# A two-layer graph attention kernel: VectorE's order beside the products of W1 is dealt anew, two weight sums trade places, a third of each W2 block is loaded earlier, and the last logit rows go into four column groups

## The chip, the core and the metric

The kernel runs on one core of a Trainium2 chip. Its metric is the time of one execution in device microseconds (us). Before the change it is 633.82 us, the median of three runs (633.66 to 633.97). The profile shown here is that of one further execution. Engines are named as in the profile: PE is TensorE (PEld its weight loads), DVE is VectorE, ACT is ScalarE, POOL is GpSimd, SP is SyncE.

## What is computed

The reference is a graph attention network of two layers over 512 nodes and 8704 edges, with a residual and a layer norm. Cut to what matters:

```python
def gat_layer(x, W, a_s, a_d, b, edge_index, concat):
    h = (x @ W).reshape(n, H, C)
    alpha_s = einsum('nhc,hc->nh', h, a_s)
    alpha_d = einsum('nhc,hc->nh', h, a_d)
    e = leaky_relu(alpha_s[src] + alpha_d[dst], 0.2)
    e = exp(e - segment_max(e, dst)[dst])
    alpha = e / (segment_sum(e, dst)[dst] + 1e-16)
    return segment_sum(h[src] * alpha[:, :, None], dst) + b
h = elu(gat_layer(x, W1, a_src1, a_dst1, b1, edges, concat=True))   # 8 heads of 768
out = gat_layer(h, W2, a_src2, a_dst2, b2, edges, concat=True)      # 1 head of 768
y = layernorm(x + out)
```

x is 512x768, W1 768x6144 (8 heads of 768 columns) and W2 6144x768 (8 blocks of 768 rows), all in float32. The numbers of edges between each pair of nodes are counted into a dense 512x512 matrix first; after that the attention is dense.

## The kernel before, in words

**Stages.** The whole kernel is one function, `gat_pass`, and the order of its instructions is written by hand: each engine runs its own list in the order in which the lines are emitted, and waits on semaphores where it needs another engine. After the counting and the first projections (up to about 92 us of the trace) a loop `for h in range(H - 1)` goes over the heads 0 to 6. For each head it emits three stages, and PE runs them one behind the other:

1. `mixed(h, ...)` (matmuls on L966): the attention matrix times head h's features, by a seven-product scheme (P1 to P7) in three columns `c`; the result goes through `elu` into gT.
2. The second product: gT times the block of W2 of head h, added into h2. For h = 0 it is `by_halves` (seven products P1 to P7 in two parts, matmuls on L409, emptied on L445 to L451); from h = 1 it is `second_by_thirds`, 15 products of 8 recorded matmuls each (matmuls on L480, emptied on L486, L491 and L493).
3. The product of x and the block of W1 of head h + 2: `by_halves` for h = 0, `project_by_thirds` for h = 1 to 5, again 15 products on L480. I call this the **third stage**. There is none for h = 6.

The last head, 7, has its own `last_mixed` (L1008), then `second` (L409), then the attention of the second layer (L1384 to L1451), and the last loop (L1472) that forms the output rows and normalises them.

**Products that share a bank.** The two 15-product schemes keep five PSUM banks, one for each chain a, x, b, y, z (`STEPS`, L455 to L458). A product adds to what stands in its chain's bank, so it may start only when the step before it on that chain has been read out (`empty`, ACT on L486 or DVE on L493). In the third stage, counted from n = 0, the order is P8 P13 P9 P2 P4 P12 P6 P0 P1 P10 P5 P14 P11 P7 P3; P14 (n = 11) and P7 (n = 13) lie on chain x, P11 (n = 12) and P3 (n = 14) on chain y. In the second product the order is P13 P2 P8 P4 P12 P9 P6 P0 P1 P14 P10 P5 P11 P7 P3, with P10 (n = 10) and P11 (n = 12) on chain y.

**What DVE does beside the products.** In the loop of the third stage (L1308 to L1327) DVE gets, between `multiply` and `empty` of product n: the sums of W1 (`sums[p]`, L170), the left and right sums of the next attention product (`sums3`, L928 to L931 and L939 to L942), two pairs of logits (`logits`, a pair of 768-wide multiply-and-accumulate instructions on L424, at n = 11 and n = 13), and the sums P2 (n = 12) and P6 (n = 14) of the next W2 block (`sums2`, L170). The sum P4 of that block was done in the third column of the next head's `mixed` (`amid`, L1241). For h = 1 alone there are also sums of x: P13 and P9 (L1076, L1073) go beside products 8 and 10 of the second product (`in_second`, L1276), P12 and P5 beside products 2 and 7 of the third stage.

**Loads of W2.** `load_second` (L197 to L210) brings a block of W2: SP loads the rows by chunks (`load_rows(k)`, six DMAs of 384 KB), and POOL issues DMAs that add (`add_up`, L133). POOL issues in order, and each waits until what it adds to has landed. The order was: rows 1, P1 added to, rows 2, P14 added to, P0, P11, P10; the last, P10, adds P1 on top and so waits for P1. P6 is P14 - P4 and P1 is P6 + P1, so DVE's P1 waits for P10 to have read its old value.

**The last logit rows.** h2's logits for the second layer come in two parts: V times gT (`add_rows` on L1384, K = 128, 2 output columns of weights, 512 moving columns, six of them over chunks c) and the logits of h2 itself, turned by a product with the identity (four of 128 columns). `rows[32 * j:32 * j + 2]` with `tile_position=(0, 32 * j)` puts such a product in the column group j of the PE array; a product with `picks` (L1416, L1418) later sums all four groups. Before, the six went to groups 0 to 2 and the four all to group 2; the bank is cleared by a memset (L1394) that `last_mixed` emits in its column c = 1.

Of the kernel before, what the change touches and what calls it, by code (L numbers as in the profile page):

```python
# [37 lines left out]
def gat_pass(  # L38
# [16 lines left out]
    nc = tc.nc  # L55
    P = 128
# [3 lines left out]
    NT = N // P  # L60
    DC = D // P
# [70 lines left out]
    def add_up(o, i):  # L132
        nc.gpsimd.dma_start(o, i, accum_op=ALU.add)  # L133
# [63 lines left out]
    def load_second(h):  # L197

        B_, part, load_rows, load_pairs, load_four, ops = thirds_of(w2[h * D:(h + 1) * D, :], "w1", w1_sums.get, w1_rows)

        def load_rest():
            load_rows(1)
            add_up(B_["P1"], part(1, 2))
            load_rows(2)
            add_up(B_["P14"], part(0, 1))
            add_up(B_["P0"], B_["P12"])
            load_four("P11", "P10")
            add_up(B_["P10"], B_["P1"])
        ops["P7"] = lambda: add_up(B_["P7"], B_["P6"])
        return B_, ops, load_pairs, lambda: load_rows(0), load_rest  # L210
# [71 lines left out]
    ident = const.tile([P, P], F32, name="ident")  # L282
# [90 lines left out]
    V = keep.tile([P, DC, 2], F32, name="V")  # L373
# [48 lines left out]
    def logits(h, feats, t):  # L422
        for al, a, sign in zip(AL[h], A[h], (1.0, -1.0)):
            nc.vector.scalar_tensor_tensor(scr, feats[:, t, :], sign, a, op0=ALU.mult,  # L424
                                           op1=ALU.mult, accum_out=al[:, t:t + 1])
# [745 lines left out]
    for h in range(H - 1):  # L1171
# [14 lines left out]
        if h == 0:  # L1186
# [25 lines left out]
            for n in range(2, 7):  # L1212
                (m0, e0), (m1, e1) = pairs[2 * n:2 * n + 2]
                m0()
                m1()
                if n < 6:
                    scored(n - 2)
                if n < 5:
                    score(n - 1)
                if n == 6:  # L1220
                    turn_in(0)
                    out_by_dma(2)
                e0()
                if 3 < n < 6:
                    out_by_dma(n - 4)
                if n == 6:
                    out_by_dma(3)
                    B2, sums2, load_pairs, load_first, load_rest = load_second(1)
                    load_pairs()
                    load_first()  # L1230
                    load_rest()
                e1()
                if n < 5:
                    fold_count(n - 1)
        else:
            G, gsums = g_thirds(h)

            def of_b(*names):
                return [sums2.pop(p) for p in names if p in sums2]

            amid = [[], of_b("P6", "P2"), behind] if h == 1 else [of_b("P1"), [], of_b("P4")]  # L1241
            finish = mixed(h, AA, BB, [[[sources[0]], [sources[1]] + amid[0]], [row, [targets[0]] + amid[1]], [amid[2], [targets[1]]]],
                           [gsums[p] for p in ("P13", "P8")])
            behind = []
# [28 lines left out]
            def also(n, *what):  # L1273
                plan[n] = plan.get(n, []) + list(what)

            for n, f in zip((8, 10), in_second):  # L1276
                also(n, f)
            if not last:
                for f in attend:
# [25 lines left out]
        if 0 < h and not last:  # L1305
            pairs = project_by_thirds(h + 2, XB, B3)
            AA, sums3 = left_sums(h + 1)
            for n in range(15):  # L1308
                pairs[n][0]()
                for p in {0: ("P6", "P2"), 1: ("P4",), 4: ("P10",), 5: ("P0",), 6: ("P1",), 9: ("P7",),  # L1310
                          12: ("P3",)}.get(n, ()):
                    sums[p]()
                if n == 5:
                    BB, rsums_ = right_sums()
                    sums3 += rsums_
                if n in (2, 3, 5, 6, 8, 9, 10):
                    for _ in range(2 if n == 8 else 1):
                        sums3.pop(0)()
                if n in (11, 13):
                    logits(h + 2, HS[h + 2], 2 + (n - 11) // 2)  # L1320
                if n in in_third:
                    in_third.pop(n)()
                if n in (12, 14):
                    sums2.pop("P2" if n == 12 else "P6")()
                pairs[n][1]()
                if n in (1, 2, 4):
                    turn_in((n + 2) // 2)  # L1327
            assert not sums3
        elif not last:
            B_, sums = right(W1[h + 2], "w2")  # L1330
            pairs = projection(h + 2, XA, B_)
            for n in range(14):
                pairs[n][0]()
                if n == 0:
                    for f in attend:
                        f()
                if n in (1, 3):
                    sums[n // 2]()
                if n == 1:
                    AA, sums3 = left_sums(h + 1)  # L1340
                pairs[n][1]()
                if n in (1, 2, 4):
                    turn_in((n + 2) // 2)
                if n == 5:
                    BB, sums3 = right_sums()
                if 1 <= n < 9:
                    sums3.pop(0)()
                if n == 0:
                    XB, early, store, late_ = x_thirds()
                if n in (2, 3, 5, 6, 7, 8, 9):  # L1350
                    early.pop(0)()
                if n == 9:
                    store()
                if n in (10, 12):
                    logits(h + 2, HS[h + 2], 2 + (n - 10) // 2)
                if n == 13:
                    late_["P10"]()
                    behind = [late_["P8"]]
                    in_second, in_third = [late_["P13"], late_["P9"]], {2: late_["P12"], 7: late_["P5"]}
        else:  # L1360
            B2, additions = sums_by_dma(W2[H - 1], w2[(H - 1) * D:, :], "w1")
            additions[0]()
            last_sum()
            additions[1]()
# [18 lines left out]
    def add_rows(lhsT, rhs, j, cols, start, stop):  # L1383
        nc.tensor.matmul(rows[32 * j:32 * j + 2, cols], lhsT, rhs, start=start, stop=stop,  # L1384
                         tile_position=(0, 32 * j), skip_group_check=True)
# [5 lines left out]

    first, second_, third_, fourth = (given(t) for t in range(NT))
    BB, rsums = right_sums()
    finish = last_mixed(AA, BB, [*rsums, lsums[3]], {(1, 0): [lambda: nc.vector.memset(rows, 0.0)], (2, 0): second_[:1], (2, 1): first})  # L1394
    every = slice(0, N)
    pairs = second(GA, B2)

# [2 lines left out]
            f()  # L1400

    run(pairs[0][0], pairs[0][1], pairs[1][0], pairs[1][1], *finish, gsums[0], gsums[1], pairs[2][0], pairs[2][1])
    for c in range(DC):
        add_rows(V[:, c, :], gT[:, c, :], c % 3, every, c < 3, c > 2 and c % 3 != 2)
    run(second_[1], pairs[3][0], gsums[2], pairs[3][1], *third_, pairs[4][0], *fourth, pairs[5][0], pairs[4][1], pairs[5][1], gsums[3],
        pairs[6][0])
    for t in range(NT):
        add_rows(al2[:, :, t], ident, 2, slice(t * P, (t + 1) * P), False, t == NT - 1)
    row2 = work.tile([P, N], F32, name="nr")
    nc.scalar.copy(row2, rows[:, :N])  # L1410
    fold(parts[:2])
# [114 lines left out]
```

## Time and profile before

| | |
|---|---|
| time, median of three runs | 633.82 us |
| time of the profiled execution | 633.37 us |
| its span, first to last instruction | 631.6 us |
| mean granted clock of TensorE | 0.996 |
| stage `mixed` of a head (h = 2 to 6) | 18.13 us |
| second product and third stage of a head (h = 2 to 5) | 52.29 us to 52.30 us together |
| second product of the last layer (`second`, from L409) to the end | 571.6 to 631.6 us |

The page of the profile gives each engine's busy time, then its share in 40 slices of the span, then the chain of work that ended last and the costliest groups. A row of the timeline has the start (us from the span's start), the time until the last of its instructions ends, the engine, the line, the operation, what it writes and reads, the shape, how many instructions it merges (xN), and in brackets the idle time of the engine before it and who ended it. Each float32 product on PE is recorded as two matmuls. PE's ends are modelled and overlap the next start, so a wait of PE is read from the starts of two rows better than from idle time.

### The profile page before, as it was taken

The page shows a single profiled execution, that of the slowest core. Times are in us where ns is not written, and L with a number is a line of the kernel's source. Part 1 is how long each engine was busy: PE and PEld are TensorE (multiplying, and loading weights), DVE is VectorE, ACT ScalarE, POOL GpSimd, SP SyncE. Part 2 cuts the span into 40 slices and gives each one's busy share as a digit, 9 for nine tenths or more (in the row PEclk, how much of TensorE's full clock was granted, in tenths as well). Part 3 has the DMA queues.
Part 4 walks back from the last instruction along what each step waited for, and adds up shares of the span by engine and source line. Part 5 has one row for each costly group of instructions (what it writes and reads, how often), then busy time and mean ns, then how long its engine had stood idle before and what let it go on. Part 6 is the DMA issues. An engine that isn't in the chain of part 4 may idle for free.

```text
span 631.6 us, 8545 instructions
## 1 busy us (share of the span) xinstructions
PE 620.3 (98%) x2761; PEld 483.1 (76%) x2761; DVE 529.3 (84%) x1129; ACT 336.7 (53%) x598; POOL 149.2 (24%) x177
## 2 busy tenths in 40 slices
PE   8999999999999999999999999999999999999995
PEld 5555576556888888888888888888888888885553
DVE  8979989888898889968898778968897878968685
ACT  5875776650658236651658146751758146754361
POOL 1300011023333224323342422323342413010000
PEclk9999999999999999999999999999999999999998
DMA  8994397789999998999999998999999994590042
GB/s 292 329 245 96 70 259 249 173 244 258 246 205 152 320 253 186 181 271 222 254 214 179 310 251 182 187 290 224 226 213 202 304 279 88 124 249 2 17 76 78
DMA packets 109568, 129.45 MB, mean 205 GB/s; under 512 B 41622, under 2 KB 90446, under 8 KB 108750
## 3 DMA queue, kind: packets, MB, share of 16 engines
q1 hardware_dynamic: 75518, 91.35, 47.2%
q0 software_dynamic: 33568, 36.90, 37.7%
q10 hardware_dynamic: 432, 0.59, 0.3%
q8 instruction: 24, 0.39, 0.3%
q14 instruction: 26, 0.21, 0.1%
HBM read 99.84 MB, written 2.90 MB: 163 GB/s over the span
## 4 chain that ended last, share of the span: by engine, by line
PE 88%; DVE 5%; DMA 4%; ACT 1%; issue 1%; SPq 1%; DVEq 0%; POOLq 0%; ACTq 0%
PE mm L480 42%; PE mm L966 17%; PE mm L409 17%; PE mm L1472 3%; DMA w2r<-in_L_gnn_W_dram 3%; PE mm L1008 3%; PE held L409 2%; PE tr L742 1%; DMA w2t<-in_L_gnn_a_dst_dram 1%; PE bc L276 1%; PE held L608 1%; PE bc L742 1%; DVE h L493 0%; PE tr L1384 0%; DVE q L645 0%
## 5 line engine op out<-in xcount | busy, mean ns | idle before, releaser
L486 ACT ACTIVATE hs<-mm 128x512 f32<-128x512 f32 x30 | 17.9, 596 | 89.3 <-PE mm L480 71.2
L966 PE MATMUL mm<-PT,hs 128*128 128x256 f32 x252 | 61.3, 379 | 0.0
L493 DVE TENSOR_TENSOR hs<-hs,mm 128x512 f32<-128x512 f32 x45 | 30.8, 685 | 27.6 <-PE mm L480 27.6
L966 PEld LDWEIGHTS mm<-PT,hs 128*128 128x128 f32 x252 | 47.8, 190 | 7.2 <-ACT u L970 0.3
L649 ACT ACTIVATE q<-q,nmax 128x512 f32<-128x512 f32 x32 | 23.1, 721 | 52.9 <-DVE nmax L645 52.8
L491 POOL DMA_DIRECT2D h<-pass x22 | 26.5, 1319 | 84.4 <-ACT pass L490 75.5
L493 DVE TENSOR_TENSOR h<-h,mm 128x512 f32<-128x512 f32 x56 | 38.3, 684 | 6.2 <-PE mm L480 5.7
L966 PE MATMUL mm<-pS,gS 128*128 128x256 f32 x168 | 43.1, 379 | 0.0
L903 ACT COPY PT<-zr 128x1024 uint16<-128x1024 uint16 x34 | 39.2, 1155 | 1.5 <-DMA zr<-pS 0.9
L480 PE MATMUL mm<-w2r,gT 128*128 128x256 f32 x160 | 37.9, 385 | 0.0
L480 PE MATMUL mm<-w2r,xT 128*128 128x256 f32 x160 | 37.8, 379 | 0.0
L133 POOL DMA_DIRECT2D w1t<-in_L_gnn_W_dram x18 | 29.4, 1658 | 29.5 <-DMA w1t<-in_L_gnn_W_dram 28.7
L966 PEld LDWEIGHTS mm<-pS,gS 128*128 128x128 f32 x168 | 31.9, 190 | 4.3
L480 PE MATMUL mm<-w1t,hs 128*128 128x256 f32 x144 | 34.2, 380 | 0.5 <-DVE h L493 0.5
L480 PEld LDWEIGHTS mm<-w2r,gT 128*128 128x128 f32 x160 | 29.6, 190 | 6.6 <-DVE hs L493 3.0
L480 PE MATMUL mm<-w1r,gS 128*128 128x256 f32 x144 | 34.0, 379 | 0.0
L480 PE MATMUL mm<-w1r,hs 128*128 128x256 f32 x144 | 34.0, 379 | 0.0
L480 PEld LDWEIGHTS mm<-w2r,xT 128*128 128x128 f32 x160 | 30.4, 190 | 4.1
L970 ACT COPY u<-mm 128x256 f32<-128x256 f32 x21 | 7.8, 371 | 45.7 <-PE mm L966 45.7
L480 PEld LDWEIGHTS mm<-w1t,hs 128*128 128x128 f32 x144 | 27.2, 190 | 4.7 <-DVE h L493 0.9
L716 DVE TENSOR_SCALAR os<-nodes,idx 128x512 bf16<-128x512 f16 x104 | 29.2, 355 | 1.4 <-PE tr L742 1.4
L480 PEld LDWEIGHTS mm<-w1r,gS 128*128 128x128 f32 x144 | 27.3, 190 | 3.7
(295 smaller groups left out, 1566.6 us busy)
## 6 DMA issues: line engine op xcount, KB each, us to landing
w2r<-in_L_gnn_W_dram SPq DMA_DIRECT2D x48, 384.0 KB
w1r<-in_L_gnn_W_dram SPq DMA_DIRECT2D x43, 384.0 KB
gT<-xd SPq DMA_DIRECT2D x5, 1280.0 KB
w1t<-in_L_gnn_W_dram SPq DMA_DIRECT2D x24, 256.0 KB
h<-pass POOLq DMA_DIRECT2D x22, 256.0 KB, 4.3
w1t<-in_L_gnn_W_dram POOLq DMA_DIRECT2D x18, 256.0 KB, 6.0
w2t<-in_L_gnn_W_dram SPq DMA_DIRECT2D x15, 256.0 KB
w2t<-in_L_gnn_W_dram POOLq DMA_DIRECT2D x15, 256.0 KB, 8.9
```

Of the source, the lines that this page charges most:

```text
L133: nc.gpsimd.dma_start(o, i, accum_op=ALU.add)
L409: nc.tensor.matmul(ps[:, :HALF], A_[p][:, k, i * P:(i + 1) * P], B_[p][:, k, :], start=start and k == 0, stop=k == HK - 1, skip_group_chec ...
L480: nc.tensor.matmul(bank[chain][:, i * TH:(i + 1) * TH], A_[p][:, k, i * P:(i + 1) * P], B_[p][:, k, :], start=first and i == k == 0, stop= ...
L486: nc.scalar.activation(out(o), ps, AF.Copy, scale=sign)
L491: nc.gpsimd.dma_start(out(o), part, accum_op=ALU.add)
L493: nc.vector.tensor_tensor(out(o), out(o), ps, op=ALU.add if sign > 0 else ALU.subtract)
L649: nc.scalar.activation(q, q, AF.Exp, bias=nmax, scale=-1.0, accum_out=dens[t])
L716: nc.vector.tensor_scalar(o, nodes, idx[:, c:c + 1], None, op0=ALU.is_equal)
L903: nc.scalar.copy(PT.rearrange("p s n -> p (s n)").bitcast(U16).rearrange("p (s n h) -> p s n h", s=NT, h=2)[:, :, t * P:(t + 1) * P, :], p ...
L966: nc.tensor.matmul(bank[p][:, :HN], A_[p][:, k, c * P:(c + 1) * P], B_[p][:, k, :], start=over is None and k == 0, stop=k == 1, skip_group ...
L1008: nc.tensor.matmul(banks[c, p][:, :HN], A_[p][:, k, c * P:(c + 1) * P], B_[p][:, k, :], start=over is None and k == 0, stop=k == 1, skip_g ...
L1472: nc.tensor.matmul(ps[:, :cols.stop - cols.start], PT[:, s, t * P:(t + 1) * P], h2[:, s, cols], start=(s == 2), stop=(s == 1))
```

## The change

No product, no transfer and no vector operation is added or taken away, except that two of the six rows of V are cut in halves; the rest is order and place.

- **Loads of W2** (`load_second`): rows 2 and the addition to P14 come ahead of rows 1 and the addition to P1.
- **h = 0, second product**: at n = 3 the first half's `empty` (L448) is emitted ahead of the ranking of the attention rows (`scored(1)`) instead of behind it.
- **P4 of the next W2 block** is no longer in `mixed`'s third column; it is the last thing of the third stage, behind P6.
- **h = 1**: the two sums of x beside the second product go from products 8 and 10 to 12 and 14.
- **Third stage**: the two left sums go to n = 1 and the others to n = 2, 6, 7, 8, 9 (before: 2, 3, 5, 6, 8, 8, 9, 10); the sums P7 and P3 of W1 go from n = 9 and 12 to 8 and 10; P2 of the next W2 block goes from n = 12 to 3, and P6 stays at 14; the four logit instructions go one each to n = 11, 12, 13, 14 (before: two at 11, two at 13).
- **Last layer**: the memset of the rows moves from `last_mixed`'s column 1 ahead of its columns, behind the sums; one logit instruction of h2's rows 128 to 255 moves from column 2 to the end of column 1; the rows of V go four whole ones to groups 0 to 3 and the two others as four halves of 256 columns to groups 0 to 3; the four turned logits go one to each group.

```diff
         def load_rest():
+            load_rows(2)
+            add_up(B_["P14"], part(0, 1))
             load_rows(1)
             add_up(B_["P1"], part(1, 2))
-            load_rows(2)
-            add_up(B_["P14"], part(0, 1))
             add_up(B_["P0"], B_["P12"])
...
                 m0()
                 m1()
+                if n == 3:
+                    e0()
                 if n < 6:
                     scored(n - 2)
...
-                e0()
+                if n != 3:
+                    e0()
...
-            amid = [[], of_b("P6", "P2"), behind] if h == 1 else [of_b("P1"), [], of_b("P4")]
+            amid = [[], of_b("P6", "P2"), behind] if h == 1 else [of_b("P1"), [], []]
...
-            for n, f in zip((8, 10), in_second):
+            for n, f in zip((12, 14), in_second):
...
+            some = [f for t in (2, 3) for f in half_logits(h + 2, t)]
             for n in range(15):
                 pairs[n][0]()
-                for p in {0: ("P6", "P2"), 1: ("P4",), 4: ("P10",), 5: ("P0",), 6: ("P1",), 9: ("P7",),
-                          12: ("P3",)}.get(n, ()):
+                for p in {0: ("P6", "P2"), 1: ("P4",), 4: ("P10",), 5: ("P0",), 6: ("P1",), 8: ("P7",),
+                          10: ("P3",)}.get(n, ()):
                     sums[p]()
...
-                if n in (2, 3, 5, 6, 8, 9, 10):
-                    for _ in range(2 if n == 8 else 1):
-                        sums3.pop(0)()
-                if n in (11, 13):
-                    logits(h + 2, HS[h + 2], 2 + (n - 11) // 2)
+                for _ in range({1: 2, 2: 1, 6: 1, 7: 2, 8: 1, 9: 1}.get(n, 0)):
+                    sums3.pop(0)()
+                for f in {11: some[:1], 12: some[1:2], 13: some[2:3], 14: some[3:]}.get(n, ()):
+                    f()
                 if n in in_third:
                     in_third.pop(n)()
-                if n in (12, 14):
-                    sums2.pop("P2" if n == 12 else "P6")()
+                for p in {3: ("P2",), 14: ("P6", "P4")}.get(n, ()):
+                    sums2.pop(p)()
                 pairs[n][1]()
...
-    finish = last_mixed(AA, BB, [*rsums, lsums[3]], {(1, 0): [lambda: nc.vector.memset(rows, 0.0)], (2, 0): second_[:1], (2, 1): first})
+    finish = last_mixed(AA, BB, [*rsums, lsums[3], lambda: nc.vector.memset(rows, 0.0)], {(1, 1): second_[:1], (2, 1): first})
...
-    for c in range(DC):
-        add_rows(V[:, c, :], gT[:, c, :], c % 3, every, c < 3, c > 2 and c % 3 != 2)
+    for c in range(4):
+        add_rows(V[:, c, :], gT[:, c, :], c, every, True, False)
+    for j in range(4):
+        c, cols = 4 + j // 2, (near, far_)[j % 2]
+        add_rows(V[:, c, :], gT[:, c, cols], j, cols, False, False)
...
     for t in range(NT):
-        add_rows(al2[:, :, t], ident, 2, slice(t * P, (t + 1) * P), False, t == NT - 1)
+        add_rows(al2[:, :, t], ident, t, slice(t * P, (t + 1) * P), False, True)
```

## The prediction

> **What bounds the kernel now.** I read the page first, then the chain of work that ended last, then the timelines of PE and DVE around the places where two products stand further apart than the pace.
>
> ```profile
> span 631.6 us, 8545 instructions
> ...
> PE 620.3 (98%) x2761; PEld 483.1 (76%) x2761; DVE 529.3 (84%) x1129; ACT 336.7 (53%) x598; POOL 149.2 (24%) x177
> ```
>
> ```profile
> 244.13 52.29 PE mm L480 x240
> 296.42 18.13 PE mm L966 x84
> ...
> 455.40 52.29 PE mm L480 x240
> ```
>
> PE is busy for 98% of the span, and in the heads the chain is PE alone. So DVE's work counts only where it holds up a product. The second row gives the pace: 18.13 / 84 = 0.2158 us a recorded matmul, 1.727 a product of eight. At that pace 240 take 51.80, but the piece takes 52.29: 0.49 is lost in it, and in its like up to 455.40. Such losses are all that a new order can win, beside the two sets of logit rows, whose PE time itself changes.
>
> **The change, part by part.**
>
> *Third stage.*
>
> ```profile
> 290.75 1.89 PE L480 MATMUL mm<-w2t,gT 128*128 128x256 f32 x8
> 292.63 3.79 PE L480 MATMUL mm<-w2r,gT 128*128 128x256 f32 x16
> 296.26 0.59 PE L966 MATMUL mm<-PT,hs 128*128 128x256 f32 x2
> ```
>
> ```profile
> 289.28 0.69 DVE L493 TENSOR_TENSOR hs<-hs,mm 128x512 f32<-128x512 f32 x1 [0.42 <-PE mm L480]
> 290.00 0.96 DVE L424 SCALAR_TENSOR_TENSOR scr<-hs,a_s 128x768 bf16<-128x768 f32 x1
> ...
> 291.89 0.68 DVE L493 TENSOR_TENSOR hs<-hs,mm 128x512 f32<-128x512 f32 x1
> 292.49 0.68 DVE L170 TENSOR_TENSOR w2r<-w2t,w2r 128x512 f32<-128x512 f32 x1
> ```
>
> The last three products (24 matmuls) take 296.26 - 290.75 = 5.51 where the pace gives 5.18: 0.33 lost. The reason stands in the second fence: product 13 starts at 292.63, 0.06 behind the end (292.57) of product 11's readout, which shares its bank and stood behind a pair of logits. Product 14 is held likewise behind the second pair's place. A busy row ends 0.16 behind its last start plus one pace (1.89 against 1.73), which I take off below.
>
> In the new order I let DVE run by these lengths (0.60 from a 512-wide operation to the next, 1.0 a logit; a readout may start 0.26 behind its product, as at 289.28, where product 11 had started at 290.75 - 1.73 = 289.02). Without the loss product 13 is due at 292.47 and 14 at 294.20. Readout 10 ends its turn at 289.9, one logit goes to 290.9, readout 11 starts at 291.0 and ends at 291.7, 0.8 ahead of product 13. The next logit goes to 292.6, readout 12 runs from 292.75 to 293.4, 0.8 ahead of product 14. Earlier, the left sums at n = 1 hold back only readout 1, needed at n = 4; t1 and t2 at n = 7 put readout 7 at 284.2 to 284.9, needed at 285.6. Everything that moved lies beside products. The last logit, P6 and P4 then fill DVE to 297.3; it is next wanted by `mixed` behind eight matmuls, at 295.93 + 1.73 and 0.1 to 0.2 more. So **0.33 in each of five heads (h = 1 to 5): 1.65**. If a sum's data came late DVE would stop for all behind it; that is the rival on loads below.
>
> *P4 out of `mixed`.*
>
> ```profile
> 241.90 0.69 DVE L170 TENSOR_TENSOR w1r<-w1t,w1r 128x512 f32<-128x512 f32 x1
> 242.50 0.42 DVE L982 TENSOR_TENSOR zr<-mm,w 128x256 f32<-128x256 f32 x1
> ```
>
> ```profile
> 244.03 1.99 PE L480 MATMUL mm<-w1t,absent 128*128 128x256 f32 x8
> ```
>
> P4 ends its turn at 242.50, and the chain through L982 to the sum that the next product needs follows without a gap; PE's product that L982 reads was over eight matmuls before the next product was due, at 244.03 - 0.06 - 1.73 = 242.24, so L982 could start at 242.44 to 242.50. The product at 244.03 shows 1.99 for eight instead of 1.89, the 0.10 that PE needs to fill up again after a wait, and it is 0.06 late itself. Bounds: nothing, or the whole 0.16. I take 0.06 for each of five heads: **0.30** (0 to 0.80).
>
> *h = 1, second product.*
>
> ```profile
> 191.97 1.89 PE L480 MATMUL mm<-w1r,hs 128*128 128x256 f32 x8
> 194.32 1.99 PE L480 MATMUL mm<-w1t,hs 128*128 128x256 f32 x8 [0.46 <-DVE h L493]
> ```
>
> ```profile
> 189.00 0.69 DVE L1076 SCALAR_TENSOR_TENSOR xT<-xT 128x512 f32<-128x512 f32 x1
> ...
> 192.99 0.69 DVE L1073 TENSOR_TENSOR xT<-xT 128x512 f32<-128x512 f32 x1
> 193.59 0.68 DVE L493 TENSOR_TENSOR h<-h,mm 128x512 f32<-128x512 f32 x1
> ```
>
> Product 12 waits for readout 10 (193.59 to 194.27): 2.35 - 1.73 = 0.62, and 0.10 to fill up: 0.72. With the two sums of x moved behind, DVE is there 1.2 earlier, at 192.4; the readout ends at 193.1, before the due 193.70. What is late next: the sum P13 now stands ahead of readout 12, so P3's sum ends only 0.1 ahead of product 14, and P5's in the third stage puts readout 7 at 0.1 ahead of product 9. Each may cost 0 to 0.2; I take 0.1 each. **0.72 - 0.20 = 0.52.**
>
> *h = 0.*
>
> ```profile
> 111.41 4.03 PE L409 MATMUL mm<-w1r,gT 128*128 128x384 f32 x12
> 115.77 1.56 PE L409 MATMUL mm<-w1t,gT 128*128 128x384 f32 x4 [0.32 <-DVE h L448]
> ```
>
> ```profile
> 115.16 1.01 DVE L448 TENSOR_TENSOR h<-h,mm 128x384 f32<-128x384 f32 x2
> ```
>
> Twelve matmuls take 4.03 - 0.16 = 3.87, the next starts after 4.36: 0.49 lost, plus 0.11 to fill up (1.56 for four, where 4 x 3.87 / 12 + 0.16 is 1.45). The readout stood behind the ranking. Its product is over at 111.41 + 3.87 / 2 = 113.35; ahead of the ranking it starts as soon as DVE is through with the operation in hand, 0.7 later at most. The ranking gets 0.47 later, and with it the exponential on ACT and the next ranking, whose rows PE wants much later. **0.60.**
>
> *`last_mixed`.*
>
> ```profile
> 563.05 1.03 PE L1008 MATMUL mm<-pS,hs 128*128 128x256 f32 x4
> 564.37 1.13 PE L1008 MATMUL mm<-PT,gS 128*128 128x256 f32 x4 [0.29 <-DVE zr L1045]
> ...
> 569.65 1.03 PE L1008 MATMUL mm<-pS,hs 128*128 128x256 f32 x4
> 570.66 1.13 PE L1008 MATMUL mm<-PT,gS 128*128 128x256 f32 x4
> ```
>
> ```profile
> 563.52 0.48 DVE L1394 MEMSET tr<- 128x512 f32 x1
> 563.91 0.41 DVE L1045 TENSOR_TENSOR zr<-mm,w 128x256 f32<-128x256 f32 x1
> ...
> 567.34 0.42 DVE L1036 TENSOR_TENSOR u<-u,mm 128x256 f32<-128x256 f32 x1 [1.37 <-PE mm L1008]
> ...
> 569.31 0.95 DVE L1388 SCALAR_TENSOR_TENSOR scr<-h,w2t 128x768 bf16<-128x768 f32 x1
> ...
> 570.19 0.42 DVE L1045 TENSOR_TENSOR zr<-mm,w 128x256 f32<-128x256 f32 x1
> ```
>
> Four matmuls need 0.86. The first gap is 1.32, the second 1.01: 0.46 + 0.15, and 0.10 twice: **0.81**. Both times L1045 is late, behind the memset and behind the logit. The logit moves into the 1.37 that DVE idles ahead of 567.34; the memset moves ahead of column 0, where its 0.48 can delay a readout of a bank that is not used again at once.
>
> *Logit rows.*
>
> ```profile
> 577.53 1.89 PE L1384 MATMUL tr<-gT,V 128*2 128x512 f32 x12
> ```
>
> ```profile
> 587.29 1.04 PE L1384 MATMUL tr<-ident,al 128*2 128x128 f32 x8
> ```
>
> ```profile
> 15.68 1.28 PE L742 MATMUL tr<-os,odw 128*32 128x512 bf16 x16
> ```
>
> Twelve matmuls in three groups take 1.73, four rounds of 0.43. In four groups there are two rounds of 0.43 and two of half length: 0.43 saved. The eight of 128 columns, all in one group, take 0.88, 0.11 each; in four groups two rounds: 0.66 saved. That four groups run side by side the third row shows, products of the counting in four groups: sixteen 512-wide ones in 1.12, 0.07 each. **1.09.** The attention that follows starts from these rows (their copy, then PE's pick, then ACT and DVE), so its chain comes earlier with PE; if it did not, PE would wait at L1472 for up to this 1.09.
>
> [...]
>
> **Sum.** 1.65 + 0.30 + 0.52 + 0.60 + 0.81 + 1.09 = 4.97. The profiled execution took 633.37 (span 631.6 and 1.8 around it); 633.37 - 4.97 = 628.40. The median shown, 633.82, is 0.45 above that execution, so I forecast **628.9**.
>
> **Rivals.**
>
> *The wait only changes its place.* DVE is busy 84% of the time; another readout or sum could be late where I count 0.7 us in hand, and the 1.65 of the third stage would stay: 630.5. Against it: the moved sums go where DVE idled for PE (0.42 ahead of 289.28).
>
> *The fourth group runs alone.* Then V's rows take 2.57 instead of 1.73, the turned ones 0.43 instead of 0.88: 0.4 lost instead of 1.09 won, 630.4.
>
> *The tail does not follow*, the edit saves PE time that PE then waits for at L1472: 630.0.
>
> *Slower: the third of W2 that is no longer loaded first.*
>
> ```profile
> 288.31 1.19 POOL L133 DMA_DIRECT2D w1r<-in_L_gnn_W_dram  x1 [9.53 <-DMA w1r<-in_L_gnn_W_dram]
> 290.21 1.20 POOL L133 DMA_DIRECT2D w1r<-in_L_gnn_W_dram  x1 [0.71 <-DMA w1r<-in_L_gnn_W_dram]
> ...
> 292.98 2.10 POOL L133 DMA_DIRECT2D w1t<-w1r  x1
> ```
>
> ```profile
> w1t<-w1r POOLq DMA_DIRECT2D x6, 256.0 KB, 7.8
> ```
>
> ```profile
> 303.71 0.69 DVE L170 TENSOR_TENSOR w1r<-w1t,w1r 128x512 f32<-128x512 f32 x1
> ```
>
> P1's addition takes the second place, 1.90 later. P10's, which needs it, may be issued up to 1.90 later too; it lands at 292.98 + 7.8 = 300.8 now, so by 302.7, and DVE's P1 waits for it at 303.4 (0.33 earlier than now). 0.7 is left. SP's six row loads are of one size, so that what follows them on SP is not moved. If the landing slipped by more than that, DVE would stop in `mixed` ahead of L976, with PE's bank behind it, in five heads. It decides against the change from (4.97 + 1.27) / 5 = 1.25 us a head, a landing 2 us beyond my bound: 635.1 and more. In its favour is only that POOL's queue is in order. [...] P10 is the last of its group; what it holds is the next head's load, and no row here shows that one pressed.
>
> **How the numbers follow.** Forecast (628.0 to 629.7): 0.76. Wait moved: 0.09. Fourth group alone: 0.03. Tail: 0.03. Slower by loads: 0.05; several losses that leave it within 0.2% (1.27 us, about what a measurement of this kernel can tell from no change): 0.04. The low end takes P4's whole 0.80 and no new wait (628.2), and 0.2 of scatter; the high end takes in the three middle rivals, 630.7. Faster 0.91, same 0.04, slower 0.05.
>
> **What would show it.** Right: the pieces of 240 matmuls at 51.9 to 52.0; product 12 of h = 1 1.73 behind product 11; 3.87 ahead of the L409 row of P4; no wait at L1008; L1384's rows 1.4 and 0.4 long. Wrong: DVE waiting for a DMA at L170, a new bracket on L480, or L1472 waiting for ACT's PT.

## The result, and the profile after

The changed kernel takes 628.92 us (median of six executions, 627.87 to 629.72); the kernel before, on the same chip, 633.74 (six, 632.79 to 634.59). The ratio is 0.9924 with a 95% interval of 0.9911 to 0.9938, so the change makes the kernel faster by 0.6% to 0.9%. The profiled execution of the changed kernel is the slowest of its six, 629.72 us; that of before took 633.37. The prediction was 628.9.

The page of the changed kernel, its span, its engines and its chain of work:

```profile
span 627.9 us, 8546 instructions
...
PE 617.0 (98%) x2765; PEld 484.1 (77%) x2765; DVE 529.7 (84%) x1129; ACT 336.4 (54%) x598; POOL 149.8 (24%) x177
...
PE 97%; DVE 1%; ACT 1%; issue 0%; DVEq 0%; ACTq 0%
```

The kernel is as PE-bound as it was. What the change won are holes between products, and they are read one by one. First the chain of waits of the changed kernel between 198 and 320 us (start, length, what):

```profile
224.70 9.51 PE mm L966 x44
...
234.78 0.43 DVE w L977
...
235.25 8.20 PE mm L966 x36
243.45 51.92 PE mm L480 x240
295.37 18.13 PE mm L966 x84
```

The piece of 240 matmuls is 51.92 long where it was 52.29, and the piece of `mixed` is as long as it was, 18.13. (The chain counts the wait at the boundary of the two to the piece of 240; the table below, which goes by the starts of the stages, counts it to `mixed`.) In head 2 the chain leaves PE once, in `mixed`, for DVE: that is new, and comes below.

The third stage and the DVE rows beside it, in the timelines of PE and of DVE:

```profile
290.03 1.89 PE L480 MATMUL mm<-w2t,gT 128*128 128x256 f32 x8
291.75 3.62 PE L480 MATMUL mm<-w2r,gT 128*128 128x256 f32 x16
295.21 1.03 PE L966 MATMUL mm<-PT,hs 128*128 128x256 f32 x4
```

```profile
290.23 0.69 DVE L493 TENSOR_TENSOR hs<-hs,mm 128x512 f32<-128x512 f32 x1
...
291.95 0.69 DVE L493 TENSOR_TENSOR hs<-hs,mm 128x512 f32<-128x512 f32 x1 [0.16 <-PE mm L480]
```

The last three products take 295.21 - 290.03 = 5.18, the pace exactly, where they took 5.51. Readout 11 now ends at 290.92, 0.83 ahead of product 13 at 291.75, and DVE waits 0.16 for PE ahead of readout 12, as the bracket says: PE is the later of the two again.

The second products of h = 1 and of h = 0, on PE:

```profile
191.67 1.89 PE L480 MATMUL mm<-w1r,hs 128*128 128x256 f32 x8
193.40 1.89 PE L480 MATMUL mm<-w1t,hs 128*128 128x256 f32 x8
```

```profile
111.70 4.03 PE L409 MATMUL mm<-w1r,gT 128*128 128x384 f32 x12
115.57 0.81 PE L409 MATMUL mm<-w1t,gT 128*128 128x384 f32 x2
```

Product 12 of h = 1 stands 1.73 behind product 11 (it was 2.35), and P4 of h = 0 3.87 behind the row ahead of it (4.36); both brackets are gone. In `last_mixed` the two places of the old brackets are now 0.86 apart, four matmuls at full pace:

```profile
560.97 1.03 PE L1008 MATMUL mm<-pS,hs 128*128 128x256 f32 x4
561.83 1.03 PE L1008 MATMUL mm<-PT,gS 128*128 128x256 f32 x4
...
567.01 1.03 PE L1008 MATMUL mm<-pS,hs 128*128 128x256 f32 x4
567.87 1.03 PE L1008 MATMUL mm<-PT,gS 128*128 128x256 f32 x4
```

The logit rows (L1387 of the changed kernel), in two stretches of PE's timeline:

```profile
574.63 1.47 PE L1387 MATMUL tr<-gT,V 128*2 128x512 f32 x16
576.04 1.24 PE L409 MATMUL mm<-w2r,gT 128*128 128x384 f32 x3
```

```profile
583.98 0.40 PE L1387 MATMUL tr<-ident,al 128*2 128x128 f32 x8
584.31 1.56 PE L409 MATMUL mm<-w2r,gT 128*128 128x384 f32 x4
```

From the first start to the next product V's rows take 1.41 (they took 579.35 - 577.53 = 1.82) and the turned ones 0.33 (0.97).

Stage by stage, by the starts of the stages on PE in the two traces, the changed kernel against before:

| stage | predicted | seen |
|---|---|---|
| second product of h = 0 | -0.60 | -0.59 |
| second product of h = 1 | -0.52 | -0.67 |
| five third stages | -1.65 | -0.33, -0.33, -0.34, -0.33, -0.32 |
| `mixed` of heads 2 to 6 (P4) | -0.30 | +0.57, -0.05, -0.04, -0.05, +0.04 |
| `last_mixed` | -0.81 | -0.76 |
| logit rows | -1.09 | -0.41, -0.64 |
| sum | -4.97 | -4.25 |

Behind the logit rows the distance to before stays at 3.95 to PE's last matmul (620.50; in before 624.45), so PE's tail follows in full. The 0.3 between 4.25 and 3.95 lies ahead of the first changed instruction: the second product of h = 0 begins at 99.98 us, 0.29 later than in before, with the same code in front. Other executions of the changed kernel begin it up to 0.9 earlier than this one. The last instruction of all is only 3.66 earlier (627.92, before 631.58). From the first matmul of the last loop (L1472, here L1478) to that instruction it is 27.98 here and 27.69 in before, and 27.7 to 28.1 in all fourteen profiles, whether the kernel's logit rows are changed or not.

**What the prediction's sum does not have** is a wait in `mixed`, above all of head 2. PE, DVE and POOL there, each from its timeline:

```profile
234.03 1.03 PE L966 MATMUL mm<-pS,gS 128*128 128x256 f32 x4
235.25 1.13 PE L966 MATMUL mm<-pS,hs 128*128 128x256 f32 x4 [0.19 <-DVE w L977]
```

```profile
231.99 0.08 DVE L418 DVE_READ_ACCUMULATOR scr<-hs,a_s 128x1 f32 x1
233.65 0.69 DVE L170 TENSOR_TENSOR w1r<-w1t,w1r 128x512 f32<-128x512 f32 x1 [1.57 <-issue]
```

```profile
224.81 1.20 POOL L133 DMA_DIRECT2D w1t<-w1r  x1 [1.38 <-DMA w1r<-in_L_gnn_W_dram]
```

The POOL row is P10's addition. The trace has it landing at 233.57, 8.76 after its issue, and 0.08 later DVE's P1 begins, after 1.57 without work; L976 and L977, which PE needs, stand behind it. PE loses 0.35 at 235.25 and 0.27 in the passes behind it, 0.62 together. In head 6 of the same execution DVE's P1 waits too:

```profile
513.94 0.69 DVE L170 TENSOR_TENSOR w1r<-w1t,w1r 128x512 f32<-128x512 f32 x1 [1.05 <-DMA w1t<-w1r]
```

PE loses 0.10 to that. DVE waiting for a DMA at L170 is one of the signs that the prediction named for being wrong. This is the place and the mechanism of the rival that was to make the kernel slower, in two heads of five, at half the price at which it decides in one of them and far below it in the other.

### The profile page after: what moved, and what is told of

It is laid out like the page before. It is cut to its first block, busy times and chain, and to the rows that moved or that the text cites. A ratio compares the mean times of both kernels' runs of the same rounds, so it can differ in the third digit from the quotient of the medians.

```text
span 627.9 us, 8546 instructions
## 1 busy us (share of the span) xinstructions
PE 617.0 (98%) x2765; PEld 484.1 (77%) x2765; DVE 529.7 (84%) x1129; ACT 336.4 (54%) x598; POOL 149.8 (24%) x177
## 4 chain that ended last, share of the span: by engine, by line
PE 97%; DVE 1%; ACT 1%; issue 0%; DVEq 0%; ACTq 0%
PE mm L480 46%; PE mm L966 20%; PE mm L409 19%; PE mm L1478 3%; PE mm L1008 3%; PE held L409 2%; PE tr L742 1%; PE bc L276 1%; PE held L608 1%; PE bc L742 1%; ACT os L714 0%; PE mm L307 0%; PE tr L1387 0%; DVE os L716 0%; DVE scr L418 0%
## 5 line engine op out<-in xcount | busy, mean ns | idle before, releaser
L480 PE MATMUL mm<-w2r,xT 128*128 128x256 f32 x160 | 37.8, 379 | 0.0
L480 PE MATMUL mm<-w2r,gT 128*128 128x256 f32 x160 | 37.0, 379 | 0.0
L480 PE MATMUL mm<-w1t,hs 128*128 128x256 f32 x144 | 34.1, 380 | 0.0
L480 PE MATMUL mm<-w1r,hs 128*128 128x256 f32 x144 | 34.1, 379 | 0.0
L480 PE MATMUL mm<-w1r,gS 128*128 128x256 f32 x144 | 34.0, 379 | 0.0
L480 PEld LDWEIGHTS mm<-w2r,gT 128*128 128x128 f32 x160 | 30.4, 190 | 4.1
L480 PEld LDWEIGHTS mm<-w2r,xT 128*128 128x128 f32 x160 | 30.4, 190 | 4.1
L480 PEld LDWEIGHTS mm<-w1t,hs 128*128 128x128 f32 x144 | 27.3, 190 | 3.9 <-ACT absent L490 0.2
L480 PEld LDWEIGHTS mm<-w1r,hs 128*128 128x128 f32 x144 | 27.2, 190 | 3.8 <-DVE hs L1127 0.2
L480 PEld LDWEIGHTS mm<-w1r,gS 128*128 128x128 f32 x144 | 27.3, 190 | 3.7
```

Source lines behind the costliest of these rows:

```text
L480: nc.tensor.matmul(bank[chain][:, i * TH:(i + 1) * TH], A_[p][:, k, i * P:(i + 1) * P], B_[p][:, k, :], start=first and i == k == 0, stop= ...
```

## The experiments

The question for the chip: do the parts bring what their holes in the trace were worth, each by itself, and is P10's landing an accident of one execution or a cost of the new load order? My theory: the parts add up, and the landing is a race that the new order tightens. The rivals: a wait only moves when one part is made alone; the new load order is worth something that I had counted at nothing. In each group of runs before is timed beside it, on the same chip.

**The changed kernel again**, unedited.

> The changed kernel once more, for a second profile on the chip of the next three. Theory (each wait of TensorE that the prediction named is gone for itself): 4.2 to 5.0 us below the kernel before, with pieces of 240 matmuls at 51.9 us. If the wait of 0.64 us in head 2's attention product (column 1, behind the sum P1 of W2) is a race between POOL's last addition and SP's next row loads, it comes again when the addition to P1 lands within some 0.3 us of the start of that product, and is gone otherwise. Rival (that wait is chance, a DMA that was slow once): it does not come again.

Measured: 628.18 us (628.08 to 628.56, five executions) against 633.28, ratio 0.9922 (0.9909 to 0.9934): 5.10 less, 0.1 more than the theory's 4.2 to 5.0. In its profile P10 of head 2 is issued at 224.03, lands at 232.24 after 8.21, and DVE's P1 waits 1.03 for it; PE loses 0.10 and not 0.62. So about 1 us of DVE's idleness is slack here, and the wait is a matter of half a microsecond.

**The changed kernel with the old load order.**

```diff
-            load_rows(2)
-            add_up(B_["P14"], part(0, 1))
             load_rows(1)
             add_up(B_["P1"], part(1, 2))
+            load_rows(2)
+            add_up(B_["P14"], part(0, 1))
```

> The changed kernel with W2's row loads and additions in the old order (rows 1 and P1 first). Theory (the new order of loads wins nothing and makes POOL's P10 wait for P1's later landing, which in head 2 costs 0.64 us): P10 is issued without a wait, head 2's attention product is 18.1 us long again, and the time is 0.3 to 0.7 us below the changed kernel. Rival (P6 and P4 at the end of the third stage need the third of W2 sooner): VectorE waits for a DMA at P6, the attention products begin late, and the time is 0.5 to 2 us above the changed kernel.

Measured: 628.38 (627.81 to 630.21, six) against 633.28, ratio 0.9930 (0.9918 to 0.9942); between the two changed kernels there is no difference that can be told. P10 of head 2 is issued at 221.06 and lands at 228.20, and DVE's P1 begins 3.0 later, without a wait. All the gains of the table stand, and with no wait in head 2 its stages add up to 4.96 less than before. So the theory held in the trace and not in the time (0.3 to 0.7 below the changed kernel was expected), and the rival did not hold: the other edits do not need the earlier third of W2, and giving it up does not show in the median.

**The third stage alone**: before with the new order of the third stage, P4 still in `mixed`, the old loads.

> The kernel before with nothing but the new order of VectorE in the third stage (P4 stays in the attention product, loads as before). Theory: the two waits at the end of the third stage go, 0.33 us in each of five heads, 1.65 us below before; pieces of 240 matmuls at 51.96 us. Rival (the waits only move to another readout of the third stage): within 0.3 us of before, the pieces still at 52.2 to 52.3 us.

Measured: 632.06 (631.20 to 633.82, eight) against 633.28, ratio 0.9984 (0.9974 to 0.9994). In the trace five third stages are 0.33, 0.33, 0.33, 0.33 and 0.32 shorter, 1.64 together, and `mixed` is unchanged, which leaves the 0.05 a head of the whole to P4. PE's timeline of this kernel:

```profile
290.25 1.89 PE L480 MATMUL mm<-w2t,gT 128*128 128x256 f32 x8
291.98 3.62 PE L480 MATMUL mm<-w2r,gT 128*128 128x256 f32 x16
295.43 0.81 PE L966 MATMUL mm<-PT,hs 128*128 128x256 f32 x3
```

295.43 - 290.25 = 5.18, the pace.

**Only the four logits dealt singly**: before, with the logits at n = 11, 12, 13, 14 and all other work of the third stage in its old place.

```diff
+            some = [f for t in (2, 3) for f in half_logits(h + 2, t)]
...
-                if n in (11, 13):
-                    logits(h + 2, HS[h + 2], 2 + (n - 11) // 2)
+                for f in {11: some[:1], 12: some[1:2], 13: some[2:3], 14: some[3:]}.get(n, ()):
+                    f()
```

> The kernel before with only the four logits of the third stage spread to products 11, 12, 13, 14; sums stay where they were, P3 and P2 both at 12. Theory (all that stands ahead of a readout counts): product 13 is no longer held (0.25 us won a head), but readout 12 now stands behind two sums and a logit, ends about 0.3 us behind the start due for product 14, and holds that one by 0.4 us in place of 0.08: between 0.2 us faster and 0.8 us slower than before over five heads. Rival (the pair of logits alone was the cause): 1.65 us faster.

Measured: 633.03 (632.52 to 634.82, eleven) against 633.28, ratio 0.9997 (0.9988 to 1.0006). PE:

```profile
290.75 1.89 PE L480 MATMUL mm<-w2t,gT 128*128 128x256 f32 x8
292.47 3.89 PE L480 MATMUL mm<-w2r,gT 128*128 128x256 f32 x16
296.20 1.03 PE L966 MATMUL mm<-PT,hs 128*128 128x256 f32 x4
```

Product 13 starts on time (292.47), but the row of products 13 and 14 is 3.89 long instead of 3.62: product 14 now waits, 0.17 and 0.10 to fill up. The last three products take 5.45, 0.05 to 0.06 less than before. This is the first rival, "the wait only changes its place", seen at work. That the pair of logits alone is the cause is refuted: DVE had too much in the last four products, and other work had to leave them too. That this is the sums P3 (from n = 12 to 10) and P2 (from 12 to 3) is my reading; no run moves them by themselves.

**The logit rows alone.**

> The kernel before with only the last logit rows in four column groups. Theory (four groups run side by side and the attention that follows comes earlier with them): V's rows 1.4 us in place of 1.8, the turned ones 0.33 in place of 0.97, 1.05 us below before. Rival (the fourth group runs alone): V's rows 2.6 us, 0.4 us above before. Rival (the tail does not follow): the rows are shorter, TensorE waits for PT ahead of the output rows, within 0.2 us of before.

Measured: 632.34 (631.94 to 632.90, eleven) against 633.38, ratio 0.9985 (0.9976 to 0.9994). In the trace 0.42 and 0.63, and PE keeps all of it to its last matmul:

```profile
576.94 1.47 PE L1384 MATMUL tr<-gT,V 128*2 128x512 f32 x16
578.35 0.91 PE L409 MATMUL mm<-w2r,gT 128*128 128x384 f32 x2
```

**`last_mixed` alone**: the memset and the logit.

> The kernel before with only the memset and one logit moved in the last head's attention product. Theory: both waits behind L1045 go, 0.76 to 0.81 us below before. Rival (the memset ahead of column 0 holds a readout there and a bank with it): less than 0.4 us, with a new wait at L1008.

Measured: 632.59 (632.03 to 633.32, eleven) against 633.38, ratio 0.9986 (0.9977 to 0.9995); 0.76 in the trace.

**Heads 0 and 1 alone**: the readout ahead of the ranking, the sums of x at products 12 and 14.

> The kernel before with only the early readout in head 0 and the two sums of x moved in head 1. Theory: 0.60 + 0.67 = 1.27 us below before; product 12 of head 1 stands 1.73 us behind product 11. Rival (the later ranking in head 0 holds the readouts behind it): head 0's second product still 27.8 us long, 0.7 us below before.

Measured: 632.26 (631.54 to 632.65, eleven) against 633.38, ratio 0.9979 (0.9970 to 0.9988); 0.59 and 0.67 in the trace.

**The new load order alone.**

> The kernel before with only the new order of W2's loads. Theory (the early third gives the old order of VectorE nothing; P10 is issued later, but still 1.2 us ahead of SP's next row loads, since without the other edits TensorE ends the third stage later): within 0.4 us of before, no wait of VectorE at P1. Rival (the third of W2 that comes sooner is what the change wins by): 1 us or more below before. Rival (P10 issued late is enough to be slow): 0.5 us or more above before, VectorE waiting at P1 in head 2.

Measured: 634.01 (633.17 to 634.62, eleven) against 633.38, ratio 1.0007 (0.9998 to 1.0016): 0.63 slower by the medians, and the interval still takes in no difference. That is more than the 0.4 of the theory; the slower rival's 0.5 is reached, but not its place: head 2 has no wait. Nothing became faster in the trace. DVE in `mixed` of head 6 in this kernel, and then in before:

```profile
516.32 0.69 DVE L170 TENSOR_TENSOR w1r<-w1t,w1r 128x512 f32<-128x512 f32 x1 [0.92 <-DMA w1t<-w1r]
```

```profile
514.99 0.69 DVE L170 TENSOR_TENSOR w1r<-w1t,w1r 128x512 f32<-128x512 f32 x1
```

In head 6 P10 comes at the last moment in before already: it lands at 514.97, DVE is there at 514.99. With the new loads DVE waits 0.92 there. A wait at this place is not peculiar to the new loads: the kernels with the logit rows alone and with `last_mixed` alone, which have the old ones, wait 0.47 and 0.61. PE does not feel the 0.92 in `mixed`, but 27 us later a product of the same head waits 0.34 for ACT (L490), whose row stands behind a ranking that is 0.36 later against PE than in before. In the two kernels with 0.47 and 0.61 that row stands where it does in before. So a slack of about 0.6 that the 0.92 exceeds would fit; that the 0.36 comes from the 0.92 is my reading and was not tried by itself.

**The changed kernel a third time**, as the yardstick for the next three.

> The changed kernel a third time, as the yardstick for the three runs beside it and as one more execution for the wait that the first profile shows in `mixed` of head 2 (0.64 us in all, behind POOL's P10 that landed 8.76 us after its issue) and the second does not (P10 landed 8.21 us after its issue). Theory (a race between the landing of P10 and DVE's P1 that is decided by fractions of a microsecond): 628.2 to 629.2 us, and a wait of 0 to 0.7 us at that place. Rival (the wait belongs to the new order of DVE and not to the landing): the wait stands at the same place and P10 lands at least 1 us before DVE reaches P1.

Measured: 628.77 (628.37 to 630.74, six) against 633.36, ratio 0.9931 (0.9919 to 0.9943). P10 of head 2 lands 6.76 after its issue, 1.77 ahead of DVE's P1, and there is no wait in head 2. In head 6 DVE waits 1.09 and PE loses 0.15. So the theory of a race holds, and the order of DVE is not the cause.

**P2 ahead of P13 in the second product**, to win what is left at that boundary.

```diff
-        return by_thirds(h2, A_, B_, ("P13", "P2", "P8", ...
+        return by_thirds(h2, A_, B_, ("P2", "P13", "P8", ...
```

> The changed kernel with P2 ahead of P13 in the second product's order (what is computed is the same). What is left at that boundary in the changed kernel is 0.107 us in each of heads 1 to 6, on the first pass of P13 over the weights that DVE or ACT finished last. Theory (the release of P13's weights comes too late for the weight load to run ahead): P2 stands there with weights that came earlier, P13 finds its own ready, and each of six heads gains 0.10 us: 0.6 us less than the changed kernel beside it. Rival (the pass after any change of stage costs 0.107 us, whatever product is first): no difference, within 0.2 us, and the 0.107 us stands on P2's first pass. Second rival (P2's weights are the later ones): 0.1 to 0.5 us more in each head, 0.6 to 3 us slower.

Measured: 628.77 (627.73 to 633.71, six), ratio 0.9927 (0.9914 to 0.9941): no gain in the median. The boundary itself does what the theory says. PE at the start of the second product of head 2 in the kernel beside it, and here:

```profile
242.42 1.99 PE L480 MATMUL mm<-w1t,absent 128*128 128x256 f32 x8
```

```profile
242.06 1.89 PE L480 MATMUL mm<-w1t,gT 128*128 128x256 f32 x8
```

1.99 for eight has become 1.89, and so in heads 1 to 5, at least 0.10 each; in head 6 another product takes the 0.10 over (at 532.81). The profiled execution is nevertheless the slowest of its six, 633.71, because of `mixed` of head 6. DVE and PE there:

```profile
516.50 0.69 DVE L170 TENSOR_TENSOR w1r<-w1t,w1r 128x512 f32<-128x512 f32 x1 [5.31 <-DMA w1t<-w1r]
```

```profile
513.15 1.03 PE L966 MATMUL mm<-pS,gS 128*128 128x256 f32 x4
518.10 2.07 PE L966 MATMUL mm<-pS,hs 128*128 128x256 f32 x4 [3.93 <-DVE w L977]
```

POOL issued P10 at 506.79 (503.23 in the kernel beside it), it landed at 516.48, and DVE stood for 5.31 us. `mixed` of this head is 23.97 long where it is 18.13 without a wait: 5.8 us, the slower rival's mechanism at more than four times the 1.25 a head at which it decides. P10 was issued late because P1's addition landed late, 7.05 after its issue and not 4.31 as in the kernel beside it; in both P10 was issued 0.54 behind that landing. Why the addition took longer no run isolates.

**P2 ahead of P13 with the old loads.**

> The changed kernel with the load order of before and P2 ahead of P13 in the second product. Theory (the load order is worth nothing here, and the boundary costs 0.107 us in each of six heads): the same time as the kernel with P2 first and the new loads, within 0.4 us, so 0.6 us less than the changed kernel; no wait in `mixed` of head 2. Rival (the load order buys the ready weights that P2 in front needs): waits of 0.1 us or more at the first product of the second product, and 0.5 us or more above the kernel with P2 first and the new loads.

Measured: 629.84 (628.22 to 630.19, five), ratio 0.9932 (0.9919 to 0.9946). No gain, and the median is 1.07 above that with the new loads, outside the theory's 0.4; the intervals of the two ratios overlap. The first product of the second product is as free of waits as with the new loads, so the rival's reason for such a loss is not seen. P10 of head 6, issued at 502.09, takes 12.15 to land; DVE waits 2.55 and PE loses 1.61. So the load order of before is no protection in head 6 either; four other kernels with the old loads wait there, 0.12 to 0.61.

**P1's addition later still**: the loads of its rows and its addition behind P11's.

```diff
             load_rows(2)
             add_up(B_["P14"], part(0, 1))
+            load_four("P11", "P10")
             load_rows(1)
             add_up(B_["P1"], part(1, 2))
             add_up(B_["P0"], B_["P12"])
-            load_four("P11", "P10")
             add_up(B_["P10"], B_["P1"])
```

> The changed kernel with the loads of P1's rows and POOL's addition to P1 put behind the addition to P11 and behind the loads of P10 and P11, in each of heads 0 to 5 (what is computed is the same). It doubles the suspected cost of the slower rival: POOL's P10 is issued 1 to 2 us later and lands later, and DVE's P1 in `mixed` waits for it. Theory (a margin of 3.0 us in heads 3 to 6, and of less than 0.5 us in head 2, that decides): a wait of 0.5 to 2 us in `mixed` of head 2, at most one other head waits, and the time is 0.5 to 2.5 us above the changed kernel. Rival of the prediction as it was put (0.7 us are left in every head): all of heads 2 to 6 wait 0.3 to 1.5 us each, 2 to 7 us above. Third: the queue takes it up, P10 lands as early as before, no difference within 0.3 us.

Measured: 631.55 (628.55 to 637.93, twelve), ratio 0.9988 (0.9963 to 1.0013). The median is 2.78 above the changed kernel, 0.3 over the theory's range and inside that of the rival (2 to 7), and the scatter has grown from 2.4 to 9.4 us. The profiled execution is the fastest of the twelve; DVE's P1 in its heads 3, 4 and 6:

```profile
302.05 0.69 DVE L170 TENSOR_TENSOR w1r<-w1t,w1r 128x512 f32<-128x512 f32 x1 [0.69 <-issue]
```

```profile
371.95 0.69 DVE L170 TENSOR_TENSOR w1r<-w1t,w1r 128x512 f32<-128x512 f32 x1 [0.54 <-issue]
```

```profile
512.96 0.69 DVE L170 TENSOR_TENSOR w1r<-w1t,w1r 128x512 f32<-128x512 f32 x1 [1.46 <-DMA w1t<-w1r]
```

The place was a miss for both: head 2 does not wait here (1.1 are left) and head 5 does not, heads 3, 4 and 6 do. PE loses nothing to the first two waits and 0.51 to the third. In which heads the slower executions lost up to 9 us more, no trace shows.

## Why the prediction was right, and where it was not

**The time and the method.** 628.9 was forecast; the changed kernel's three medians are 628.92, 628.18 and 628.77. That the first lies 0.02 from the forecast is luck: the medians scatter by 0.7, and the sum of 4.97 comes so close to the 4.96 of the trace without a wait in `mixed` (the changed kernel with the old loads) because 0.15 too little for h = 1 makes up for some 0.05 too much in each of P4, `last_mixed` and the logit rows. The method is not luck. The working was a sum of holes read off one trace, and each hole that it counted closed, but for what is said below; the part alone, in the trace and by the medians, against the term:

| part | term | whole, trace | alone, trace | alone, medians |
|---|---|---|---|---|
| third stage | 1.65 | 1.65 | 1.64 | 1.22 |
| h = 0 and h = 1 | 1.12 | 1.26 | 1.26 | 1.12 |
| `last_mixed` | 0.81 | 0.76 | 0.76 | 0.79 |
| logit rows | 1.09 | 1.05 | 1.05 | 1.04 |
| load order | 0 | (head 2) | -0.36 | -0.63 |

Each median carries about 0.6 us of uncertainty (the interval of its ratio), so the trace, which has the place, is the sharper witness. P4 was not run alone.

**Third stage.** Right in its size and in the working by 0.6 and 1.0 us steps: readout 11 was to end 0.8 ahead of product 13 and ended 0.83 ahead. The run with the logits alone shows that it had to be worked through to product 14: closing the hole that the profile shows would have opened the next one.

**P4.** The lower of the two effects, 0.06 a head, was taken and seen (0.05) wherever nothing else came in. The 0.10 of filling up stays: 1.99 at the head of each second product. The run with P2 in front shows what it hangs on: not on the change of stage but on P13, whose weights come just in time (PEld waits 0.3 at most for DVE's L1130, six times in the changed kernel).

**h = 1.** Mis-sized: 0.20 was taken off for two waits that might arise, and the trace has one of 0.06, at the end of the second product, and none in the third stage. **`last_mixed` and h = 0** are right to 0.05.

**Logit rows.** The fourth group runs beside the other three: V's sixteen recorded matmuls take 1.41, four in a group, and the turned ones 0.33. "The fourth group runs alone", an assumption with no row of before behind it, is refuted, in the whole and alone (1.41 both times, not 2.57), and so is "the tail does not follow": the 1.05 stands unchanged at PE's last matmul, and alone it gives 1.04 by the medians.

**Loads: the step that failed.** The rival's working said that P10 lands 7.8 after its issue, "so by 302.7", and that "0.7 is left", in five heads alike. Each of the three figures was one number for what differs from head to head and from execution to execution. In the changed kernel's profile the same DMA landed 8.8, 5.6, 4.2, 5.5 and 10.1 us after its issue in heads 2 to 6; the margin to DVE's P1 was none in head 2, 3.0, 5.1 and 4.8 in heads 3 to 5, and none in head 6. Head 3, from which I took the 0.7, does not wait in any of the three profiles of the changed kernel. Head 6 had no margin in before already, and the working left it out. In head 2 the old order leaves 3.0 to 5.3 us in the eight kernels that have it, the new one none to 3.0 in the five with the load order as it was changed. The first half of the working, that P1's place in the order sets when P10 is issued, is shown: in every head of all fourteen profiles P10 is issued 0.28 to 0.55 behind the landing of P1's addition. So the mechanism of the slower rival is real and in head 2 the new load order feeds it; in head 6 both orders wait, five of the eight kernels with the old one and all five with the new one. What I got wrong is how often it would act at all: it cost 0.7 us in the first profiled execution of the change (heads 2 and 6), 5.8 in one of a kernel close to it. The price of one missed landing has no bound in the sum, because PE simply stands (3.93 us without work ahead of 518.10 in the latter).

**What it says of the change as a whole.** Of its parts the load order alone brought nothing that a trace or a median shows. A version without it (the changed kernel with old loads) is level with the changed kernel, not faster; no version here beats it by more than the medians scatter.

## What to carry to other kernels

When an engine is the bound from end to end, read its holes one by one as distances between starts, name the engine that fills each, and play the new order through until that engine waits for the bound one again; dealing away the visible wait alone may only hand it to the next product. For a DMA that another engine waits for, read issue, landing and need in every head, not the median of the group: the head with no margin decides, and it can show in the scatter before it shows in the median. An edit of which no wait in the trace says what it is for is worth running alone.

## What the runs showed of the hardware

The landing of one and the same 256 KB addition by POOL took from 4.2 to 12.2 us across these kernels. Of heads 2 to 6, head 6, where SP issues six row loads of 384 KB around it, is the slowest in each (9.0 to 12.2). The DMA view of the changed kernel, for P10 of head 2, which was issued 0.08 us behind the first of SP's six row loads:

```profile
L133 POOL DMA_DIRECT2D w1t<-w1r x1: 1199/1199/1199, 224.8 to 224.8; - x1
...
DMA to landing us min/median/max: 8.8/8.8/8.8
```

In before the same DMA of head 2 was issued 3.0 us ahead of those loads and landed after 5.0. That the row loads slow it fits both, and was not isolated. In heads 2 to 5 of the five kernels with the changed load order the fit goes on: 8.2 and 8.8 where SP's first row load is issued 0.1 ahead of P10, 4.2 to 6.0 where it is issued 2.0 or more behind it. With the old order it does not: in head 3 the first row load comes 2.0 to 4.3 behind P10, and the landing takes 6.5 to 8.4 all the same. So the row loads alone do not set it.

A long stand of PE cost more than itself in the one case on record. In the kernel with P2 in front PE stood from about 514 to 518 us; the stretches around it, with the granted clock in the column behind the five engines' busy times (PE, PEld, DVE, ACT, POOL):

```profile
505.00:513.00 8.00, 8.00 (x39) 7.04 (x38) 4.22 (x11) 3.44 (x9) 2.47 (x2) 1.00 1.11 302
514.00:518.00 4.00, 0.17 (x1) 0.00 (x0) 1.40 (x4) 1.30 (x4) 0.00 (x0) 1.00 1.11 296
518.20:521.40 3.20, 3.20 (x8) 2.57 (x9) 1.97 (x6) 0.00 (x0) 0.00 (x0) 0.50 0.68 133
522.00:527.00 5.00, 5.00 (x25) 4.39 (x24) 3.48 (x9) 4.30 (x10) 0.00 (x0) 1.00 0.17 52
```

For 3.2 us behind the wait the granted clock is 0.50, and the matmuls start 0.427 apart instead of 0.216: about 1.8 us on top of the 4.1 waited, the fill-up included. The shorter stand with the old loads (1.34 us) left the granted clock at 1.00 and the matmuls behind it at 0.216.

And weights that PE gets just in time still cost 0.10 us: the distance from the first matmul to the next is 0.320 instead of 0.216. PE's row has no idle time in it; there it shows only as 1.99 for eight matmuls instead of 1.89. The weight loads (PEld) show it: in the changed kernel they wait six times for DVE's L1130 ahead of L480, 1.6 us together, and with P2 in front that wait is gone, and in heads 1 to 5 the 0.10 with it.
